# GpSimd's low halves of weights behind the first layer norm, and new constants for a written-out order

## The chip, the cores and the metric

The kernel runs on one core of a Trainium2 chip. The metric is the device time in microseconds (us) of one execution. Beside it stand readings from one profiled execution: its span, from the first to the last instruction, and the busy time of each engine. The engines are PE (matrix products), ACT (activations), DVE (vector operations), POOL (GpSimd, vector operations too, slower) and SP, which here only issues transfers.

## What is computed

A block of four residual layers over eight sequences of 512 tokens with 128 channels, everything in 32-bit floats:

```python
x = x + ssm(layernorm(x))        # 128x128 in, 3-tap convolution, a scan over 512 tokens
x = x + ffn(layernorm(x))        # 8 experts, all of them for every token
x = x + attention(layernorm(x))  # 16 heads of 8, tokens see their chunk of 10 and 25 before their own place
x = x + ffn(layernorm(x))        # the same experts again
```

The part that takes most of the time is the expert layer, used twice:

```python
g = einsum('bsh,ehf->ebsf', x, w_gate)      # 8 experts, 128 -> 512
u = einsum('bsh,ehf->ebsf', x, w_up)
h = silu(g) * u
y = einsum('ebsf,efh->ebsh', h, w_down)     # 512 -> 128
cw = softmax(x @ w_router) * softmax(x @ w_gating / 0.1)
out = einsum('ebsh,bse->bsh', y, cw / (sum(cw) + 1e-9))
```

The first layer is a scan: with `decay` and `drive` of shape (tokens, 64, 8), `state = decay * state + drive`, and the output of a token is the sum of `state * c` over the 8 states plus `D * x`.

## The kernel before

**Products.** A product of 32-bit accuracy is made of three fast ones (`matmul3`): each operand is split into a high half (a cast to the type fp32r) and a low half (what the cast left out), and high x high, low x high and high x low are summed in one bank. So each of the 24 weight tiles of the experts (`wg`, `wu`, `wd` for 8 experts) is loaded as `stage...`, its high half cast by ACT, and its low half taken by a subtraction, on GpSimd at first, on GpSimd or DVE later (`lows`, lines 987 to 1000). Every hidden tile `h` is split in the same way: `h0...` of four or two products, `h00`/`h01` its high half, `h10`/`h11` its low half.

**The order.** All instructions of all engines are written out by the program itself while it is built. `Clock` keeps, in Python, an account of when each engine would be free: `cost` says what an instruction is charged, `run` where it goes, and for transfers (key `S`) when the data would be there. `Lanes` holds generators, one per chain of work; a `yield "V", t` says that the next instructions need DVE and data that is there at `t`; a `yield` of a function waits for a condition. `tick` takes the lane that can start first. The order on each engine is then fixed, and the chip keeps to it, with semaphores between the engines. So a constant of the account changes no arithmetic, but it may change the place of any instruction on any engine.

**The stages.** The scan of sequence 0 is done first and in two halves of 256 tokens (`first_halves`, half `c` = 0 and 1), so that the expert layer can start with the first half. `scanned` is one such half: `decays` computes softplus and exponentials on ACT (`delta`, `mdec`), `clips` bounds them on DVE, `steps` multiplies and scans (`mst`), `mcx` weighs the states, and `mo` are the products of the output. Then `ffn_prep` normalises (`layernorm`: statistics `st`, `mv` on DVE, `va` and `rs` on GpSimd, `xn` on DVE), transposes (`tp`), splits (`xt0`, `xt1`), and computes the router's weights (`lps`, `rps`, `cps`, `cw`), which go to memory and come back spread over the partitions (`cwb`).

Until the first half is ready PE has nothing else to do and is kept busy with products `warm` that nobody reads (line 1750 and on). Later such products, then called `idle`, are put in by `keep_warm` when the account finds PE free for over `WARM_GAP` (0.25 us) in the first one and a half sequences.

The expert layer is one stream (`ffn_stream`): for each sequence, for each expert, for each quarter of 128 of the 512 hidden channels, a `g`, a `u` and, some steps later, a `y`, three products of 512 columns each. Of sequence 0 the first experts, `SPLIT` of them, are passed twice, with 256 tokens each time and two quarters at once (six products of 256 columns). Six banks hold `g`, `u` and `y`; the rest of the eight belong to the side chains. Beside the stream run the scans of the sequences 1 to 7 (`mamba_front`, `mamba_back`), the preparation of the next expert layer (`ffn_preps`) and the attention (`attention_preps`, then `attention`). `due` functions and `MAMBA_DUE` and `PREP_DUE` say from which position in the stream a chain is pressing, `SIDE`, `JOIN` and `JOIN_ATT` how long a chain's products wait to join others on PE, `HELD` how much a chain is held back while PE is starved.

**The gate on the low halves.** The first `EARLIEST` = 10 weight tiles have their low halves taken before the first layer norm where time allows. A set of names in `done` steers them: "halves" lets them start, "quiet" stops them. "quiet" is set when the layer norm of the first half begins to be issued, and taken away when its output is split. While "quiet" is there, the second half's DVE steps wait too (`undisturbed`).

Of the kernel before, what the change touches and what calls it, by code (L numbers as in the profile page):

```python
# [87 lines left out]

TABLES = {AF.Silu: (18,), AF.Exp: (0, 6), AF.Ln: (6,), AF.Tanh: (0, 18)}
INF = float("inf")  # L90
LAGS = {"T": 0.2, "A": 0.15, "V": 0.15, "P": 0.08}
TO_PE = 0.11
SAME = 0.125
# [1 line left out]
EDGE = 0.1  # L95
FIRST = 0.6
LATE = 0.3
SIDE = 0.5
JOIN = 2.0
JOIN_DUE = 0.0  # L100
JOIN_MAX = 6.0
JOIN_ATT = 3.0
JOIN_END = 2.0
MOST = 6
OTHERS = 4
# [3 lines left out]
WARM_TO = 1.5  # L109
SECOND = 0.2  # L110
PRESS = 0.4
HELD = 0.18
MAMBA_DUE = 0.9
PREP_DUE = 0.9
ATT_LEAD = 2.5
EARLY = 5
SPLIT = 4
EARLIEST = 2 * (DEPTH + 1)


# [8 lines left out]
class Clock:  # L129
# [105 lines left out]
    def run(self, key, name, out, args, kw, after, wait):  # L235
        c = self.cost(key, name, out, args, kw)
        start = max(self.end[key] + wait, after, self.now if key == "T" else self.based(key))
        if key == "T":
            if start > self.end["T"] + 2.4:
                self.cold = start  # L240
            if start < self.cold + 3.4:
                c *= 2
        if key in "VP" and self.shares(key, name, out, args):
            start = self.with_port(start, c)
        self.end[key] = start + c
        if key == "S":
            start = max(start, self.now)
            row = out.shape[-1]
            rows = out.shape[0] * size(out) // row
            each = max(row * (2 if out.dtype == BF16 else 4), 512)  # L250
            move = rows * each / 200e3
            self.moved = max(self.moved, start + c + 0.8) + move
            return self.moved + 0.6 + move
        self.hop[key] = start + c
        return start + c + LAGS[key]

# [23 lines left out]
class Lanes:  # L280
# [39 lines left out]
    def start(self, lane):  # L320
# [3 lines left out]
        if callable(need):  # L324
            return 0.0 if need() else INF
        if need == "T":
# [51 lines left out]
def block_kernel(ctx: ExitStack, tc: tile.TileContext, x, pack_a, pack_b, pack_c, w_qkv, mask, mask_t, w_o,  # L378
                 w_gate, w_up, w_down, out):
    nc = tc.nc  # L380
    clock = Clock()
# [21 lines left out]
    done = {}  # L403
# [163 lines left out]
    def table(name, number):  # L567
        if clock.table != number:
            nc.scalar.preload_act_table_set(name)
            clock.table = number  # L570
            clock.end["A"] = max(clock.end["A"], clock.now) + 1.28
# [63 lines left out]
    first = lambda gen: lanes.hurry(gen, FIRST)  # L635
# [69 lines left out]
    def first_halves(sb, consts, h, xo):  # L705
# [39 lines left out]
        def scanned(c, pbc, pde):  # L745
# [37 lines left out]
            def decays():  # L783
                yield "V"

                e = freed(dve.tensor_scalar(delta, pde, bdt, LN_E_1, ALU.add, ALU.min))
                yield lambda: issued["tanh"] == 2
                yield "A", e
                nega = consts["nega"]
                table("natural_log_exp_and_others", 6)  # L790
                act.activation(delta, delta, AF.Exp)
                act.activation(delta, delta, AF.Ln, bias=1.0)
                for p in range(2):
                    yield "A"
                    dec = sb.tile([P, 2, HALF], F32, tag="dec", name=f"mdec0_{c}_{p}", bufs=5)
                    for i in range(2):

                        decs["t", p, i] = act.activation(
                            dec[:, i], delta, AF.Exp, scale=nega[:, 2 * p + i : 2 * p + i + 1]
                        )  # L800
                    decs[p] = dec
                if c:
                    table("exp_and_others", 0)
# [53 lines left out]
            for p in range(2):  # L857
# [6 lines left out]
                for t in range(2):  # L864
                    for i in range(2):
                        pe.matmul(
                            ops[t], cx[:, i, t * P : (t + 1) * P], pa[:, A_WOUT : A_WOUT + P],
                            start=False, stop=(p == i == 1),
# [88 lines left out]
    def ffn_weights(sb):  # L957

        todo = [(e, nm, src) for e in range(NE) for nm, src in (("g", w_gate), ("u", w_up), ("d", w_down))]
        stages = {}  # L960

        def load(i):
            e, nm, src = todo[i]
            if i < EARLIEST:

                t = fp.tile([P, L], F32R, tag=f"h{i % 2}", name=f"stage{nm}{e}", bufs=DEPTH + 1).bitcast(F32)
            else:
                t = qp.tile([P, FF], F32, tag=("t0", "t1", "rest")[i % 3], name=f"stage{nm}{e}")
            if nm == "d":
                end = sp.dma_start(  # L970
                    out=t.rearrange("p (c h) -> p c h", c=NFC),
                    in_=src[e].rearrange("(c p) h -> p c h", p=P),
                )
            else:
                end = sp.dma_start(out=t, in_=src[e])
            stages[i] = t, end + 1.5

        def loads():
            for i in range(3, len(todo)):
                if i > EARLIEST + 2:  # L980
                    yield lambda: i - 3 in split
                    yield "S", split[i - 3]
                load(i)

        split = {}

        def lows():
            for i, (e, nm, _) in enumerate(todo):
                yield lambda: i in stages and len(stages[i]) == 3
                yield lambda: "halves" in done and "quiet" not in done if i < EARLIEST else "first" in done  # L990
                t, there, _ = stages.pop(i)
                hi, lo = wgt[nm, e]
                yield "PV" if "first" in done else "P", there
                engine = quicker(L, W_BIAS) if "first" in done else pool
                split[i] = engine.tensor_tensor(lo, t, hi.bitcast(F32), ALU.subtract)
                done[nm, e] = 0.0
            done["weights"] = 0.0

        for i in range(3):
            load(i)  # L1000
        sp.dma_start(out=pb, in_=pack_b)
        lanes.add(loads())
        lanes.add(lows())
        for i, (e, nm, _) in enumerate(todo):
            yield lambda: i in stages
            t, there = stages[i]
            if e == EARLY:
                yield lambda: "first" in done
            yield "A", there
            stages[i] = t, act.copy(wgt[nm, e][0], t), True  # L1010
# [12 lines left out]
    def ffn_prep(k, b, xc, t0=0, nt=NT):  # L1023
# [11 lines left out]
        *_, xf = yield from normalised(xc, nm, halves, nt, t0 + nt == NT, quick=nt < NT, plain=True)  # L1035
        if (k, b, t0) == (0, 0, 0):
            done.pop("quiet", None)
            done["calm"] = 0.0
        if t0 == 0:
            done["cw", k, b] = dram.tile([NE, NT, P], F32, tag="cwd", name=f"cwd_{nm}", bufs=3), 0.0, 0  # L1040
# [678 lines left out]
    with mctx:  # L1719
        sb = msb  # L1720
        mc = {}

        def late(part):
            return lambda: pos[0] >= turn[part] - MAMBA_DUE

        def fronts(seqs):
            for b in seqs:
                turn["front"] = b
                xc = first_x
                if b:  # L1730
                    xc = yield from load_x(b, 0, f"m{b}")
                    yield lambda: ("front", b - 1) in done
                yield from mamba_front(b, sb, mc, xc)
                done["front", b] = 0.0

        def backs(seqs):
            for b in seqs:
                turn["back"] = b
                yield lambda: b in handed and (b - 1, 1) in done
                yield from mamba_back(b, sb, mc, lambda gen: lanes.add(gen, due=late("back")))  # L1740

        first(fronts(range(1)))
        first(mamba_consts(sb, mc))
        lanes.add(ffn_weights(sb))
        clock.hold = INF

        warm = now(side([P, L], "warm"))
        while (0, 0) not in ready or ready[0, 0][1] == 0:
            if lanes.tick():
                continue  # L1750
            if clock.now > WARM:
                sel = mc["sel"]
                e = pe.matmul(warm[:, :HALF], sel[:, 0], sel[:, : HALF // P], start=True, stop=True)
                clock.end["T"] += 0.1
            else:
                clock.now += 0.03
        freed(e)

        done["first"] = 0.0
        lanes.add(backs(range(1, B)), due=late("back"))  # L1760
        lanes.add(fronts(range(1, B)), due=late("front"))
        lanes.add(ffn_preps(), rank=0, due=lambda: pos[0] >= turn["prep"] - PREP_DUE)
        lanes.add(attention_preps(), rank=QRANK, joins=JOIN_ATT)
        stream = ffn_stream()

        def keep_warm():

            if pos[0] < WARM_TO and clock.now > clock.end["T"] + WARM_GAP and lanes.are_free("bank"):
                t, = take("experts", [[P, L]], ["idle"])
                sel = mc["sel"]  # L1770
                freed(pe.matmul(t[:, :HALF], sel[:, 0], sel[:, : HALF // P], start=True, stop=True), "experts")

        while "weights" not in done or (B - 1, 1) not in done:
            if next(stream):
                lanes.idle()
                keep_warm()
            else:
                lanes.tick()
# [85 lines left out]
```

## Time and profile before

| | |
|---|---|
| median of 3 runs | 1352.26 us (1350.01 to 1354.05) |
| the profiled execution's own time | 1351.71 us |
| its span | 1349.9 us |
| granted clock of PE, mean | 0.996 |
| first product of the expert layer (`g`) starts at | 34.25 us |
| products of PE | 98% of the span |

A time is read as "start, duration, engine, line, operation, out<-in". Almost every instruction has line 269, as one helper issues them all; they are told apart by the names of their tiles. The names in the profile leave numbers out: `h<-h` may be any of the hidden tiles. In square brackets stands how long the engine had been idle before and what it had waited for. In the lists of waits the columns are the total, the count and the longest.

### The profile page before, as it was taken

Reading aid. Unit: us, or ns where it says so; the run is one execution under the profiler, and the core shown is the slowest. Engines: PE = TensorE matmul, PEld = TensorE weight load, DVE = VectorE, ACT = ScalarE, POOL = GpSimd, SP = SyncE. Lnnn points to the kernel's source line nnn. Section 1 sums busy time; section 2 is a strip of 40 time slices with the busy share of each in tenths; the row PEclk is TensorE's granted clock in tenths of the full one; section 3 lists DMA queues with packets and bytes.
Section 4 is the critical chain, followed back from the end, with each engine's and each line's share of the span. In section 5 each row is a group of like instructions: output and inputs, shape, how many; then the busy total and the mean of one; then the engine's idle time right before and its main releaser. Section 6 shows DMA issues by size and latency. Waiting matters only on the chain.

```text
span 1349.9 us, 29483 instructions
## 1 busy us (share of the span) xinstructions
PE 1328.8 (98%) x10261; PEld 1053.4 (78%) x10261; DVE 1038.5 (77%) x3114; ACT 964.2 (71%) x1694; POOL 941.4 (70%) x1042
## 2 busy tenths in 40 slices
PE   7999999999999999999999999999999999999998
PEld 7877778788788877777777777777777777778886
DVE  6887888688888877897788887888888787845443
ACT  7768576867787556776777777777877767765654
POOL 5877576776767757676766767767677676777776
PEclk9999999999999999999999999999999999999999
DMA  4320303232111261344344453344443434121111
GB/s 126 95 82 28 87 24 101 64 80 76 42 48 56 63 86 52 72 102 113 79 102 114 98 125 88 95 110 102 104 99 96 114 76 102 47 71 53 40 40 40
DMA packets 182204, 107.74 MB, mean 80 GB/s; under 512 B 86401, under 2 KB 162088, under 8 KB 182056
## 3 DMA queue, kind: packets, MB, share of 16 engines
q1 hardware_dynamic: 182056, 105.87, 31.6%
q8 instruction: 81, 1.33, 0.4%
q14 instruction: 67, 0.55, 0.1%
HBM read 77.64 MB, written 27.79 MB: 78 GB/s over the span
## 4 chain that ended last, share of the span: by engine, by line
PE 91%; ACT 2%; issue 2%; POOL 2%; DVE 1%; POOLq 0%; DVEq 0%
PE u L269 26%; PE g L269 25%; PE y L269 25%; PE ao L269 2%; PE aw L269 2%; PE as L269 2%; PE mo L269 1%; POOL h L269 1%; PE aqk L269 1%; ACT h L269 1%; DVE h L269 1%; PE aout L269 1%; PE mde L269 1%; PE yp L269 1%; PE tp_f L269 0%
## 5 line engine op out<-in xcount | busy, mean ns | idle before, releaser
L269 POOL TENSOR_TENSOR h<-h,h 128x512 fp32r<-128x512 f32 x492 | 639.8, 1309 | 280.0 <-ACT h L269 223.2
L269 PE MATMUL u<-xt_f,wu 128*128 128x512 f32 (+1 forms) x1584 | 451.4, 395 | 3.6 <-ACT h L269 2.7
L269 PE MATMUL g<-xt_f,wg 128*128 128x512 f32 (+1 forms) x1584 | 448.4, 393 | 2.1 <-ACT h L269 1.9
L269 PE MATMUL y<-h,wd 128*128 128x512 f32 (+1 forms) x1584 | 445.6, 392 | 1.4 <-POOL h L269 0.8
L269 DVE TENSOR_TENSOR h<-u,h 128x512 f32<-128x512 f32 x420 | 285.8, 686 | 157.7 <-PE u L269 109.8
L269 ACT ACTIVATE h<-g 128x512 f32<-128x512 f32 x512 | 303.4, 597 | 124.8 <-PE g L269 100.6
L269 ACT CAST h<-h 128x512 fp32r<-128x512 f32 x437 | 268.3, 618 | 169.2 <-DVE h L269 167.6
L269 PEld LDWEIGHTS g<-xt_f,wg 128*128 128x128 f32 x1584 | 288.5, 189 | 70.2 <-ACT h L269 3.0
L269 PEld LDWEIGHTS y<-h,wd 128*128 128x128 f32 x1584 | 288.3, 188 | 70.3 <-POOL h L269 1.5
L269 PEld LDWEIGHTS u<-xt_f,wu 128*128 128x128 f32 x1584 | 286.7, 189 | 71.5 <-ACT h L269 4.1
L269 POOL TENSOR_TENSOR acc<-acc,cwb 128x512 f32<-128x512 f32 (+1 forms) x114 | 148.0, 1298 | 52.1 <-DVE cwb L269 44.9
L269 ACT ACT_TABLE_LOAD x109 | 139.8, 1283 | 25.2 <-PE g L269 23.7
L269 DVE CUSTOM_DVE_ANT_0 amasked<-as,maskq 128x60 f32<-128x60 f32 x640 | 95.3, 213 | 4.9 <-PE as L269 4.6
L269 DVE TENSOR_TENSOR cwb<-y,cwb 128x512 f32<-128x512 f32 (+1 forms) x116 | 77.4, 668 | 14.1 <-PE y L269 13.6
L269 DVE TENSOR_TENSOR apt<-aw,maskk 125x400 f32<-125x400 f32 (+2 forms) x160 | 88.1, 570 | 0.0
L269 DVE SCALAR_TENSOR_TENSOR h<-h,g 128x512 f32<-128x512 f32 x92 | 62.3, 681 | 28.3 <-ACT h L269 27.8
L269 ACT ACTIVATE apt<-apt 125x400 f32<-125x400 f32 (+2 forms) x160 | 81.5, 540 | 0.4
L269 DVE SCALAR_TENSOR_TENSOR h<-u,h 128x512 f32<-128x512 f32 x92 | 62.5, 683 | 3.3 <-PE g L269 0.5
L269 DVE DVE_READ_ACCUMULATOR2_ANT amx<- 128x1 f32 x640 | 51.9, 81 | 0.0
L269 DVE CAST h<-h 128x512 fp32r<-128x512 f32 x75 | 50.6, 675 | 1.2
L269 DVE COPY v<-avr 125x128 f32<-125x128 f32 (+2 forms) x40 | 25.5, 638 | 26.5 <-PE ao L269 26.0
L269 PEld LDWEIGHTS ao<-apt,v 125*32 125x32 f32 (+2 forms) x1280 | 27.4, 109 | 14.6 <-DVE h L269 4.0
(205 smaller groups left out, 1241.4 us busy)
## 6 DMA issues: line engine op xcount, KB each, us to landing
cwb<-cwd_f SPq DMA_DIRECT2D x124, 256.0 KB
aqd<-apc SPq DMA_DIRECT2D x32, 192.0 KB
ks<-aqd SPq DMA_DIRECT2D x48, 93.8 KB
x_fo<-x SPq DMA_DIRECT2D x16, 256.0 KB
aqd<-apc SPq DMA_DIRECT2D x32, 128.0 KB
x_f<-x SPq DMA_DIRECT2D x15, 256.0 KB
qs<-aqd SPq DMA_DIRECT2D x48, 75.0 KB
aod<-aos SPq DMA_DIRECT2D x24, 100.0 KB
```

The lines of the kernel that those rows point to most:

```text
L269: f(*args, **kw)
```

## The change

Three things are changed.

A second name, "still", stops the first ten low halves as "quiet" does. It is set when the exponentials of half 0 are issued, so earlier than "quiet", and taken away with it. It doesn't hold the second half's DVE steps.

The account of a transfer: before, it was there at (start + issue + 0.8, or the end of the one before) + move, + 0.6 + move; now at (start + issue + 0.6, or the end of the one before) + move, + 0.8. For 256 KB `move` is 1.31 us and the issue is charged with 0.55.

The constants: a filler `warm` is charged with its own cost and 0.02 us more instead of 0.1 (`FILL`); `SIDE`, `JOIN_ATT`, `HELD`, `MAMBA_DUE`, `PREP_DUE` have new values; `SPLIT` is 5 instead of 4, so that expert 4 of sequence 0 is passed in two halves as well.

```diff
+FILL = 0.02
-SIDE = 0.5
+SIDE = 0.6
-JOIN_ATT = 3.0
+JOIN_ATT = 8.0
-HELD = 0.18
-MAMBA_DUE = 0.9
-PREP_DUE = 0.9
+HELD = 0.15
+MAMBA_DUE = 1.0
+PREP_DUE = 0.8
-SPLIT = 4
+SPLIT = 5
...
-            self.moved = max(self.moved, start + c + 0.8) + move
-            return self.moved + 0.6 + move
+            self.moved = max(self.moved, start + c + 0.6) + move
+            return self.moved + 0.8
...
+                if c == 0:
+                    done["still"] = 0.0
                 table("natural_log_exp_and_others", 6)
                 act.activation(delta, delta, AF.Exp)
...
-                yield lambda: "halves" in done and "quiet" not in done if i < EARLIEST else "first" in done
+                yield lambda: "halves" in done and not {"quiet", "still"} & done.keys() if i < EARLIEST else "first" in done
...
             done.pop("quiet", None)
+            done.pop("still", None)
...
-                clock.end["T"] += 0.1
+                clock.end["T"] += FILL
```

## The prediction

> **What bounds the kernel now.** I read the page first, then the table of windows by stage, the waits of PE, and the timeline of the first 80 us. From the page and from the windows:
>
> ```profile
> PE 1328.8 (98%) x10261; PEld 1053.4 (78%) x10261; DVE 1038.5 (77%) x3114; ACT 964.2 (71%) x1694; POOL 941.4 (70%) x1042
> ```
>
> ```profile
> 0.00:34.20 34.20, 26.89 (x175) 23.95 (x175) 21.54 (x57) 25.10 (x54) 18.62 (x29) 0.95 0.40 125
> 34.20:100.00 65.80, 62.80 (x413) 54.32 (x414) 55.30 (x121) 46.74 (x84) 51.91 (x60) 0.97 0.31 86
> 100.00:200.00 100.00, 96.15 (x438) 74.62 (x437) 77.87 (x163) 73.38 (x125) 68.29 (x73) 0.98 0.17 50
> 300.00:400.00 100.00, 100.00 (x479) 79.93 (x478) 84.28 (x163) 77.90 (x135) 67.33 (x67) 1.00 0.20 57
> ```
>
> The columns are the window, its length, the busy time of PE, PEld, DVE, ACT and POOL, and the granted clock. From 300 us on PE is never free, so a new order can win nothing there but cheaper changes of shape. What can move lies in the first 200 us, where PE idles and its granted clock falls to 0.95 to 0.98; "busy" there also counts 111 `warm` and 30 `idle` products that compute nothing. The waits of PE say who is late:
>
> ```profile
> PE u L269 <- ACT h L269: 2.7, 3, 1.5
> PE mbx L269 <- DVE mst L269: 2.6, 1, 2.6
> ```
>
> The timeline ahead of the first expert product `g` (start, duration):
>
> ```profile
> 23.33 0.80 PE L269 MATMUL mbx<-mbc,sel 128*128 128x256 f32 x2 [2.57 <-DVE mst L269]
> 24.56 1.91 PE L269 MATMUL mo<-pa,mcx 128*128 128x128 f32 x8
> ...
> 27.54 1.05 PE L269 MATMUL mo<-pa,mcx 128*128 128x128 f32 x8
> 28.34 3.00 PE L269 MATMUL warm<-sel 128*128 128x256 f32 x23
> 28.88 1.29 POOL L269 TENSOR_TENSOR wd<-staged,wd 128x512 fp32r<-128x512 f32 x1
> 29.23 0.30 DVE L269 BATCH_NORM_AGGREGATE mv_f<-st_f 128x2 f32<-128x6 f32 x2
> 30.25 0.19 POOL L269 TENSOR_SCALAR va_f<-mv_f 128x2 f32<-128x2 f32 x1
> 31.77 0.50 PE L269 MATMUL tp_f<-ident,xn_f 128*128 128x128 f32 x2 [0.43 <-DVE xn_f L269]
> ```
>
> The statistics are there at 29.53, but GpSimd starts `va_f` only at 30.25, behind the low half `wd`: 0.72 us that the new gate aims at. The eight `mo` at 24.56 take 1.91 us, those at 27.54 take 1.05: the first stand behind a wait of 2.57 us and run at half rate. Inside the first expert block:
>
> ```profile
> 61.74 0.88 PE L269 MATMUL g<-xt_f,wg 128*128 128x256 f32 x6
> 62.46 0.88 PE L269 MATMUL u<-xt_f,wu 128*128 128x256 f32 x6
> ...
> 64.53 1.28 ACT L569 ACT_TABLE_LOAD   x1
> ...
> 68.36 2.15 PE L269 MATMUL idle<-sel 128*128 128x256 f32 x5 [0.86 <-DVE cwt_f L269]
> 69.88 1.28 ACT L269 ACT_TABLE_LOAD   x1
> 70.56 1.45 PE L269 MATMUL u<-xt_f,wu 128*128 128x256 f32 x6
> 71.17 1.58 ACT L269 ACTIVATE h<-g 128x512 f32<-128x512 f32 x3
> ```
>
> Six products are 0.72 us from start to start when they flow. `g` of 61.74 gets its Silu only at 71.17, since ACT loads four tables between 61.08 and 71.16 and does the exponentials of sequence 1 between them; PE runs out of work at 68.2 and then creeps at half rate (0.43 us per `idle`, where 0.117 is usual).
>
> **The change, part by part.** The build gives the new order of every engine; durations are those of the rows above.
>
> *Gate and fillers, up to the first `g`.* Low halves `wg2`, `wu2`, `wd2` go behind the layer norm, so `va_f` no longer waits: at most 0.72 us sooner. But FILL makes fillers cheaper in the kernel's account, and `warm` goes from 111 to 159, 0.117 us each. Nine more stand ahead of the first `tp_m` and `mh`, where the chain has little slack: I take +0.2 us there and +0.1 before the first `mbx`. Twelve more stand inside the wait of 2.57 us, which leaves 1.2 us: no half rate, so `mo` is 0.86 us shorter and the second `mo` starts with its data (27.2 instead of 27.54). Then 31 instead of 23 stand before `tp_f`: 31 x 0.117 = 3.6 us from 28.2, so `tp_f` starts at 31.85 although its data is there at 31.2. The fillers eat the gate's gain. Four more before `lps` add 0.3; the four `mo` and the `idle` that now follow it (33.36 to 34.2) move behind, 0.9 less. First `g` at 33.75 instead of 34.25: **-0.5 us**; bounds -1.3 (no filler in the way) and +0.6 (no half rate saved).
>
> The skill page TensorE: Matmul & The Clock Gate, "Part 1: The HAM clock gate", puts the fall to half rate after an idle window of about 3.4 us. The row shows it after 2.57 us. By the page the fillers inside that wait would save nothing and the start would be about +0.3 us instead of -0.5.
>
> *SPLIT 5, with the new order up to expert 5.* Before, 65.3 us pass from the first `g` (34.25) to the first `g` of expert 5 (99.57). The products in them, each at its usual start-to-start time, are 288 of 256 columns at 0.117, 41 of 512 at 0.235, 16 `mo` at 0.22 and 2.5 us of small ones: 49.4 us. So 15.9 us were fillers, waits and half rate. After, the order has 342 of 256 columns, 11 of 512, 18 `mo` and about 2 us of small ones: 48.6 us. Its waits I worked out queue by queue:
> - GpSimd starts six lows at 31.5 (1.3 each), then `h10` of the first hidden tile: 40.6. The small router steps stand behind it, so `cps_f` is ready at 42.3, while PE reaches it at 40.05. This is a new wait of 2.25 us, and what is queued behind `cps_f` on PE is the first `y`. Then `mo` waits for DVE's `mcx` (46.4) and `y` for GpSimd (46.6). PE reaches the second half at about 62.1: 28.4 us for 23.1 of products, 5.3 lost, against 5.7 before.
> - From there to expert 5, 10.2 us were lost before. Now the exponentials of sequence 1 and of the router share one table load, and the Silu of the second half follows one more: two loads of 1.28 fewer in this stretch. From its own load to that Silu ACT needs 7.3 us, and PE has 8.4 us of products ahead of the first that needs the bank. Expert 4's five extra groups are that cover; without it PE would stand about 3 us as it does now. I take 1.5 us lost here, and 3.2 up to expert 5 where `wd7` and its neighbours come sooner in GpSimd's queue.
>
> Together about 10 us instead of 15.9: **-5.9**, and 0.8 fewer products. Bounds: -11 if half of the 10 goes too, +2 if the new wait costs as the one at 68 did.
>
> The skill page ScalarE: Activation LUTs, "What ACT_TABLE_LOAD costs", gives about 2.66 us per switch with its drain; the rows show 1.28 and the next activation 0.01 us behind. By the page the two loads would be worth 5.3 us instead of 2.6.
>
> *What is pushed behind.* Products of the side chains that stood before expert 5 come after it: total product time after the first `g` is 1284.9 us against 1284.6, so +1.0 from expert 5 on, and the 0.8 above is given back.
>
> *Constants in the rest.* A shape change costs PE 0.11 us (518.2 us: 0.34 to the second product of `u`, 0.232 usual). Pricing the whole order by such pairs gives -2 to +1 from the second sequence on: 0. Thirteen casts go from ACT (0.62) to DVE (0.43) under a full PE: 0. The two extra half steps of expert 4 (DVE 0.41, GpSimd 0.73, one transfer) lie beside PE.
>
> *Account of transfers.* The first `x` is issued at 0.72 and used at 3.71, 3.0 us. The account charged 4.6 and now charges 3.3, so users are queued 1.3 us sooner but not too soon. SP sends `cwd` and the `cwb` of the first half ahead of the store of `x0`; the waits of DVE, ACT and GpSimd name a DMA only for that first `x`, so 0. If that cover goes, the price is 1.3 us each time in front of DVE.
>
> Sum: -0.5 - 5.9 - 0.8 + 1.0 = -6.2 us. The waits inside the block were worked out with undisturbed durations, while DVE's clips beside a GpSimd low took 0.57 and 0.87 us instead of 0.33; for this I keep about three quarters: -4.5. The profiled execution is 1351.7 (span 1349.9 and 1.8 around it), 0.6 below the median of 1352.26. So **1347.5**; by itself 1344 to 1350.
>
> **The rivals.**
> - *GpSimd's backlog decides (slower).* Three lows, 3.9 us, now stand ahead of every `h10`. If GpSimd is the last to release PE through the first block, PE trails by 3.9 and runs 2 us longer at half rate after the wait for `cps_f`: +5.9 - 0.5 - 1.4 (12 `idle` fewer) = +4.0, 1355.7. It decides once GpSimd has under 3.9 us free before the second half; it was busy 20.6 of 26 us from 34 to 60, so 5.4 were free, which speaks against it.
> - *A new stall later (no change).* Before, one wait of 1.94 us at 174 (`u`, `g` behind ACT's exponentials) was followed by products at 0.43 instead of 0.23 up to 179: 3.9 us in all. The second sequence's side work is now denser by 1.0 us. One such stall more: 1351.
> - *All of it (faster still).* Waits fall to 5 us: 1342. For it: PE's products would allow it. Against: DVE is busy 22.4 of 26 us from 34 to 60.
> - *The gate does nothing,* as fillers hold `tp_f`: this is in my sum.
>
> **How the numbers follow.** Forecast 0.45, faster still 0.12, no change by a new stall 0.20, backlog 0.23. Runs spread by 0.3% (1350.0 to 1354.1), about what can be told from no change: 1348.2 to 1356.3 is "same". Of the forecast a quarter ends in "same", of the backlog a third: faster 0.46, same 0.34, slower 0.20; as uncounted mishaps only add time I move 0.08 from same to slower. Range 1341.5 to 1357: the bounds of the block on one side, the backlog on the other.
>
> **What would show it.** `va_f` within 0.2 us of its statistics, `tp_f` behind `warm` and not behind DVE; the `mo` before 25 us in about 1 us; first `g` near 33.75; a wait at `cps_f` near 40 to 42; the first `g` of expert 5 near 93 to 95; from 300 us on full PE in every window. I am wrong if expert 5 starts after 98, or if a wait over 1.5 us appears after 130 that was not there.

## The result, and the profile after

The changed kernel takes 1364.67 us in the median of 6 runs (1362.07 to 1365.96), the kernel before 1351.61 in 6 runs beside it: a ratio of 1.0094, 95% interval 1.0079 to 1.0108. It is 13 us slower. Forecast were 1347.5 us, with a range of 1341.5 to 1357, so the prediction was wrong.

First the lines of after that answer to those shown of before: the page's line of busy times, the windows by stage, and of PE's waits the four longest of real products for ACT and the one of `mbx`.

```profile
PE 1336.9 (98%) x10333; PEld 1059.1 (78%) x10333; DVE 1039.3 (76%) x3135; ACT 951.1 (70%) x1664; POOL 946.4 (69%) x1048
```

```profile
0.00:36.30 36.30, 32.35 (x218) 30.05 (x218) 21.20 (x55) 24.89 (x54) 15.01 (x26) 1.00 0.38 118
36.30:100.00 63.70, 58.27 (x421) 52.55 (x420) 57.76 (x119) 40.36 (x75) 51.38 (x56) 0.97 0.27 79
100.00:200.00 100.00, 97.69 (x456) 76.45 (x455) 70.67 (x147) 69.75 (x127) 69.04 (x78) 0.98 0.18 51
200.00:300.00 100.00, 95.92 (x437) 74.32 (x436) 83.81 (x160) 75.07 (x130) 68.88 (x69) 1.00 0.25 69
300.00:400.00 100.00, 98.44 (x463) 77.96 (x462) 87.59 (x168) 75.16 (x128) 67.42 (x67) 1.00 0.27 72
```

```profile
PE y L270 <- ACT h L270: 2.3, 3, 1.4
PE u L270 <- ACT h L270: 2.1, 2, 1.3
PE g L270 <- ACT h L270: 1.9, 2, 1.7
PE aw L270 <- ACT h L270: 1.7, 1, 1.7
PE mbx L270 <- DVE mst L270: 1.0, 1, 1.0
```

The share of PE is 98% in both, so the first line tells nothing. The windows do: from 300 to 400 us PE had no free time before, and now 1.6 us of it; from 200 to 300 it has 4.1, where it had 1.5 before:

```profile
200.00:300.00 100.00, 98.55 (x454) 78.77 (x453) 78.18 (x147) 73.15 (x126) 69.72 (x68) 1.00 0.30 82
```

The wait of `mbx` near 24 us fell from 2.6 to 1.0 as expected; all of PE's waits for ACT come to 11.1 us, against 7.7 before.

The start, from the timeline of after (start, duration):

```profile
6.98 2.08 PE L270 MATMUL warm<-sel 128*128 128x256 f32 x8
27.28 1.05 PE L270 MATMUL mo<-pa,mcx 128*128 128x128 f32 x8
30.58 3.96 PE L270 MATMUL warm<-sel 128*128 128x256 f32 x31
32.16 0.20 POOL L270 TENSOR_SCALAR va_f<-mv_f 128x2 f32<-128x2 f32 x1 [11.75 <-DVE mv_f L270]
34.38 0.38 PE L270 MATMUL tp_f<-ident,xn_f 128*128 128x128 f32 x2
36.34 0.98 PE L270 MATMUL g<-xt_f,wg 128*128 128x256 f32 x6
```

The gate does what it says: GpSimd is idle for 11.75 us and starts `va_f` with its data. Yet the first `g` stands at 36.34, 2.1 us later than before, in an execution whose first products went at half rate (eight `warm` took 2.08 us, and 1.19 before). Two kernels that have the same order here start it at 33.92 and 33.88, so the change does not bring the delay; the last section comes back to it.

To see where time is lost I split both runs at the first `g` of a sequence's expert 0 and of its expert 4. A stage's loss is its length less its products, each at its usual start-to-start time as in the prediction. It may be negative, where shapes flow better than their mean. Each column is one execution; the three profiles that share the changed kernel's order in the second row lose 6.2, 5.9 and 6.0 us there.

| loss of PE in us | before | after | constants alone | gate alone | new account alone | after with the old account | one nudge (`h_lag_pe`) |
|---|---|---|---|---|---|---|---|
| first `g` to sequence 1 | 17.9 | 15.4 | 13.8 | 19.2 | 19.8 | 16.0 | 15.4 |
| sequence 1, experts 0 to 3 | 1.5 | 6.2 | 8.0 | 7.8 | 7.3 | 8.6 | 6.2 |
| sequence 1, experts 4 to 7 | 3.4 | -0.3 | -0.1 | 1.1 | 2.2 | -0.1 | -0.2 |
| sequence 2, experts 0 to 3 | -0.7 | 5.2 | 5.9 | 2.0 | 0.6 | 3.0 | 5.2 |
| from there to sequence 5 | -1.0 | 0.1 | 6.3 | 11.5 | 1.8 | -0.7 | 0.1 |
| sequence 5 to the second expert layer | 1.5 | 3.6 | 1.3 | 1.3 | 2.0 | 0.8 | 2.0 |
| second expert layer | 2.8 | 7.1 | 5.3 | 6.0 | 4.7 | 5.5 | 5.0 |
| sum | 25.4 | 37.3 | 40.5 | 49.0 | 38.5 | 33.0 | 33.8 |

Before and after: the first block loses 2.5 us less, which just makes up for the late start (sequence 1's first `g` stands at 129.17 against 129.01). Then 4.7 and 5.9 us go in the two stages of experts 0 to 3, against 3.7 won between them, and some 7.5 us behind expert 4 of sequence 2. The other columns are explained below.

**What stands at 133 to 145 us.** ACT and PE in the timeline of after:

```profile
132.23 0.60 ACT L270 ACTIVATE h<-g 128x512 f32<-128x512 f32 x1 [0.96 <-PE g L270]
132.84 1.28 ACT L570 ACT_TABLE_LOAD   x1
134.14 1.30 ACT L270 ACTIVATE mdelta<-mdelta 128x512 f32<-128x512 f32 x2
135.99 1.95 ACT L270 ACTIVATE mdec<-mdelta,nega 128x512 f32<-128x512 f32 x3
138.71 1.28 ACT L270 ACT_TABLE_LOAD   x1
140.01 1.57 ACT L270 ACTIVATE h<-g 128x512 f32<-128x512 f32 x3
140.66 0.82 PE L270 MATMUL idle<-sel 128*128 128x256 f32 x2 [1.76 <-ACT h L270]
141.54 1.65 PE L270 MATMUL u<-xt_f,wu 128*128 128x512 f32 x3
```

This is the picture that the prediction showed of before at 61 to 71 us: ACT changes its table, does the exponentials of a scan, changes back, and does no Silu in between, here for 7.2 us. PE runs dry, waits 1.76 us, and then the products go at half rate, at a granted clock of 0.50 from 141.5 to 144.9 us: 1.65 us for three where 0.86 is usual. These are the decay exponentials `mdec` of sequence 2's scan. Before, they stood here:

```profile
118.95 1.28 ACT L569 ACT_TABLE_LOAD   x1
120.24 1.95 ACT L269 ACTIVATE mdec<-mdelta,nega 128x512 f32<-128x512 f32 x3
123.11 1.28 ACT L269 ACT_TABLE_LOAD   x1
```

That is within sequence 0, 8.8 us ahead of sequence 1's first `g` (129.01). In the changed kernel they come 6.8 us behind it (129.17). Those of sequence 3's scan moved from 171.0 to 211.1, from 42 us ahead of sequence 2's first `g` to 1 us ahead. Before, PE waited 1.94 us behind them, up to 176.6; after has no wait over 1.5 us there, which goes with the 3.7 us won. What the new place does on DVE shows in the timeline of after some us later:

```profile
221.85 0.62 ACT L270 CAST h<-h 128x512 fp32r<-128x512 f32 x1 [1.90 <-DVE h L270]
222.33 0.69 DVE L270 SCALAR_TENSOR_TENSOR mbx<-mdec,mbx 128x512 f32<-128x512 f32 x1
222.55 1.27 POOL L270 TENSOR_TENSOR h<-h,h 128x512 fp32r<-128x512 f32 x1 [3.48 <-ACT h L270]
223.53 1.21 DVE L270 TENSOR_TENSOR_SCAN mst<-mdec,mbx 128x512 f32<-128x512 f32 x1
223.86 0.60 ACT L270 ACTIVATE h<-g 128x512 f32<-128x512 f32 x1 [1.38 <-POOL h L270]
224.51 0.97 PE L270 MATMUL g<-xt_f,wg 128*128 128x512 f32 x3 [1.66 <-ACT h L270]
```

It is read from the bottom: PE's `g` waits for a bank that ACT empties, ACT for a hidden tile that GpSimd releases, GpSimd for ACT's cast, and the cast for DVE's `h`, while DVE works on the scan. The four scans `mst` of sequence 3 start within 12 us (216.3 to 228.3); before they were spread over 41.5 us (184.5 to 226.1).

**What stands behind 570 us.** The chain of waits of after names a transfer, `x` for the attention's layer norm, three times (start, and the time from issue to use):

```profile
569.47 6.93 DMA x_a<-x
...
829.39 6.05 DMA x_a<-x
...
917.48 6.64 DMA x_a<-x
```

The engines' waits for transfers:

```profile
DVE st_a L270 <- DMA x_a<-x: 8.3, 5, 3.2
DVE st_f L270 <- DMA x_f<-x: 2.9, 2, 2.3
DVE cwb L270 <- DMA cwb<-cwd_f: 2.6, 3, 1.1
```

All of DVE's waits for transfers come to 20.3 us, against 5.1 before, of which 3.7 is the very first load. Before's transfers of `x_a` were hardly quicker, 5.8 to 6.6 us from issue to use in the three where it can be read; but its DVE came to them later, and waited for one alone:

```profile
DVE st_a L269 <- DMA x_a<-x: 0.9, 1, 0.9
```

### The profile page after: what moved, and what is told of

It reads as the page before. It is cut to its first block, busy times and chain, and to the rows that moved or that the text cites. A ratio compares the mean times of both kernels' runs of the same rounds, so it can differ in the third digit from the quotient of the medians.

```text
span 1363.7 us, 29669 instructions
## 1 busy us (share of the span) xinstructions
PE 1336.9 (98%) x10333; PEld 1059.1 (78%) x10333; DVE 1039.3 (76%) x3135; ACT 951.1 (70%) x1664; POOL 946.4 (69%) x1048
## 4 chain that ended last, share of the span: by engine, by line
PE 87%; DVE 3%; ACT 3%; issue 2%; DMA 2%; POOL 2%; SPq 0%; POOLq 0%; ACTq 0%; DVEq 0%
PE u L270 24%; PE y L270 24%; PE g L270 24%; PE ao L270 2%; PE aw L270 2%; PE as L270 2%; DMA x_a<-x 1%; PE mo L270 1%; POOL h L270 1%; ACT h L270 1%; PE warm L270 1%; DVE h L270 1%; PE aqk L270 1%; PE yp L270 1%; ACT mdec L270 0%
## 5 line engine op out<-in xcount | busy, mean ns | idle before, releaser
L270 ACT CAST h<-h 128x512 fp32r<-128x512 f32 x424 | 260.6, 619 | 194.7 <-DVE h L270 193.4
L270 ACT ACT_TABLE_LOAD x107 | 137.3, 1283 | 28.1 <-PE g L270 24.5
L270 DVE TENSOR_TENSOR cwb<-y,cwb 128x512 f32<-128x512 f32 (+1 forms) x117 | 77.5, 663 | 14.7 <-PE y L270 10.2
L270 DVE CAST h<-h 128x512 fp32r<-128x512 f32 x88 | 54.1, 618 | 1.3
L270 PE MATMUL ao<-apt,v 125*32 125x100 f32 (+2 forms) x1280 | 36.4, 254 | 0.0
```

What stands on the lines that cost most here:

```text
L270: f(*args, **kw)
```

## The experiments

Theory A: the new account lets DVE stand in front of transfers that have not landed. Theory F: the cheaper fillers cost the start. Theory S: the constants only shuffle the order, before's order happens to be a good one, and a new one loses some us by its own stalls, whatever led to it. Later a rival C stands against S: the change's parts do harm by what they are.

### Parts taken out, or put in alone

Four kernels: the changed one with the old account of transfers, and with the old charge for fillers; the kernel before with the new account alone, and with the gate alone.

```diff
 # a_old_account, in the changed kernel
-            self.moved = max(self.moved, start + c + 0.6) + move
-            return self.moved + 0.8
+            self.moved = max(self.moved, start + c + 0.8) + move
+            return self.moved + 0.6 + move
 # a_old_fill, in the changed kernel
-FILL = 0.02
+FILL = 0.1
 # b_new_account, in the kernel before: the first hunk the other way round
 # b_gate, in the kernel before
+                if c == 0:
+                    done["still"] = 0.0
...
-                yield lambda: "halves" in done and "quiet" not in done if i < EARLIEST else "first" in done
+                yield lambda: "halves" in done and not {"quiet", "still"} & done.keys() if i < EARLIEST else "first" in done
...
+            done.pop("still", None)
```

> The changed kernel with the old account of transfers, all else as changed. Theory A (transfers charged too little put DVE in front of landings; its queue stands and PE runs dry): 6 to 9 us less than the changed kernel, about 1357, and DVE's waits for a DMA behind the first x gone. Theory F (fillers cost the start): no more than 1 us less. Theory S (every new order loses some us by its own stalls, whatever the constant): anywhere from 1350 to 1365, with stalls in places that have nothing to do with transfers.

> The changed kernel with fillers charged as before. Theory F: the first g at 33 to 34 instead of 36.3, and 2 to 3 us less, about 1362. Theory A: 0 to 2.5 less, the waits for x_a stay. Theory S: 1350 to 1365 with another set of stalls.

> The kernel before with the new account of transfers alone. Theory A: 1357 to 1361, DVE waits 5 to 15 us in all for DMAs, x_a above all. Theory F: 1351 to 1352. Theory S: 1350 to 1360, waits for DMAs no more than one in three of the loss.

> The kernel before with the earlier gate on the low halves alone. Theories A and F: va_f starts within 0.2 us of its statistics, first g 0.3 to 0.9 us sooner, 1350 to 1352. Theory S: up to 5 us from before either way, by stalls behind the first g.

| kernel | median, us | ratio to before (95%) | DVE's waits for transfers, us |
|---|---|---|---|
| after, old account | 1360.91 | 1.0068 (1.0053 to 1.0083) | 5.7 |
| after, old charge for fillers | 1361.80 | 1.0070 (1.0055 to 1.0085) | 17.9 |
| before, new account | 1366.63 | 1.0103 (1.0082 to 1.0125) | 20.1 |
| before, gate | 1374.83 | 1.0168 (1.0136 to 1.0201) | 6.4 |

The account's waits follow the account. With the new one in the kernel before:

```profile
DVE st_a L269 <- DMA x_a<-x: 9.5, 6, 2.4
DVE cwb L269 <- DMA cwb<-cwd_f: 5.1, 3, 2.3
```

and with the old one in the changed kernel:

```profile
DVE st_a L270 <- DMA x_a<-x: 0.8, 2, 0.4
```

The five kernels with the new account wait 16.9 to 22.4 us in all, the fifteen with the old one 4.9 to 10.2. So theory A is right that the new account puts DVE in front of transfers. It is not the whole: the old account gives back 3.8 us of 13, where theory A expected 6 to 9, and the gate, which has nothing to do with it, costs 23 us alone. The old charge for fillers gives 2.9 us, what theory F expected. The new account alone and the gate alone came out above every range that was stated for them, theory S included (1361 and 1357 at most). The parts cost 14 and 23 us alone and 13 together with all others, so these numbers belong to the orders that came out and not to the parts.

### The order held, one part put in

To see a part's direct effect, the planner keeps its books as before and only the emitted instructions differ. Gate: the three low halves `wg2`, `wu2`, `wd2` are charged where they stood, and emitted behind the copy of `va_f`; nothing but GpSimd's queue changes. Fillers: 46 more `warm` (111 become 157), not charged; nothing but PE's queue changes.

```diff
 # e_gate_fixed
-                split[i] = engine.tensor_tensor(lo, t, hi.bitcast(F32), ALU.subtract)
+                if i in (6, 7, 8):
+                    split[i] = engine.charge("tensor_tensor", lo, t, hi.bitcast(F32), ALU.subtract)
+                    moved_lows.append((lo, t, hi.bitcast(F32), ALU.subtract))
+                else:
+                    split[i] = engine.tensor_tensor(lo, t, hi.bitcast(F32), ALU.subtract)
...
+            if tag == "f0_0_0":
+                for args in moved_lows:
+                    nc.gpsimd.tensor_tensor(*args)
 # e_fill_fixed, behind each filler
+                fills += 1
+                if fills > 19 and fills % 2:
+                    nc.tensor.matmul(warm[:, :HALF], sel[:, 0], sel[:, : HALF // P], start=True, stop=True)
```

> The order before is kept on every engine and transfer queue but GpSimd's, where only the low halves of wg2, wu2 and wd2 move from ahead of the first layer norm's copy, subtraction and power to just behind them; the planner's books are as before. What it tells is the gate's own direct effect, without a new order. By the prediction's step on the start: the statistics end at about 32, so the first product `g` comes at most as early as the full gate brought it, 1.7 us sooner (32.51 against 34.25 in the run with the gate alone); the three lows come about 1.5 to 2 us later, and expert 2's first use is not until some 20 us on, so nothing waits for them. Theory S (the gate is harmless or a small gain, and the 23 us that it cost alone are a new order's stalls far behind): 1350 to 1352, 0 to 1.7 us faster than before. Its rival G (lows taken late hold up the experts after): over 1356.

> The order before is kept on every engine, and only TensorE gets more fillers: behind every second filler from the 20th on one more, which the planner is not charged for (111 fillers become 157). Theory F (more fillers of 0.07 to 0.13 us each delay real work at the start, as in the changed kernel, where the first `g` comes 2.1 us later): the first `g` comes 1 to 3 us later and the time goes up by as much, 1353 to 1355. Theory S (fillers fit into gaps that the order leaves; the changed kernel's late start comes from its other order there): the first `g` within 0.7 us of 34.25 and the time within 0.7 us of before, 1351 to 1352.5. A granted clock that stays higher in the first 30 us could make it 0.5 us faster.

Gate: 1351.22 us, ratio 1.0006 (0.9994 to 1.0017). Fillers: 1352.04 us, ratio 0.9998 (0.9989 to 1.0006). Neither interval leaves out 1. Four of the gate's twelve executions took about 1356 us, at a mean granted clock of 0.994 where the others have 0.996 to 0.999, and what sets them apart is not on record.

The first `g` came at 35.76 with the gate and at 37.51 with the fillers, 1.5 and 3.3 us behind the 34.25 of before. But in both the first 11 us went at half rate, as in `e_press`, a kernel with before's order there (next part), whose first `g` stands at 36.51: against that one the gate brings it 0.75 us forward and the fillers put it 1.0 back, in one execution each. By sequence 2 the delay against before is 1.2 and 1.5 us, and the medians don't show it. So fillers may delay the start by about a microsecond, as theory F has it, but the time doesn't go up by as much.

The account of transfers and the five constants that only steer the planner can do nothing at a held order. `SPLIT` also changes the shapes of products, and no run held the order for it. So gate, fillers and account cost nothing by themselves that the medians show: what they cost, they cost through the order that is written. For `SPLIT` that is not shown.

### Nudges that mean nothing

Nine kernels are the one before with one number of the planner moved a little, two are the changed kernel so moved.

```diff
-PRESS = 0.4            # e_press, and f_after_press
+PRESS = 0.41
-AHEAD = 0.2            # e_ahead, and f_after_ahead
+AHEAD = 0.205
-SIDE = 0.5             # f_before_side
+SIDE = 0.52
-HELD = 0.18            # g_held
+HELD = 0.185
-start + c + 0.8) + move          # g_account_nudge
+start + c + 0.81) + move
-MAMBA_DUE = 0.9        # g_mamba
+MAMBA_DUE = 0.91
-LAGS = {"T": 0.2, "A": 0.15, "V": 0.15, "P": 0.08}
+LAGS = {"T": 0.21, "A": 0.15, "V": 0.15, "P": 0.08}    # h_lag_pe; 0.19 in h_lag_pe_down
+LAGS = {"T": 0.2, "A": 0.15, "V": 0.16, "P": 0.08}     # h_lag_dve
```

> Before, with one planner constant that the change does not touch moved by a fortieth: PRESS 0.4 to 0.41. The order is that of before up to about 110 us and another one behind. Theory S (before's order is one that came out well among many alike, and any new order costs some us by its own stalls, whatever led to it): 1355 to 1370, and new TensorE waits of 1 to 3 us in places behind 110 us. Theory A (before's constants are good, and the loss is owed to what the change does to them, to the account of transfers above all): within 3 us of before, 1349 to 1355.

> Before, with another planner constant that the change does not touch moved by a fortieth: AHEAD 0.2 to 0.205. The order is that of before up to about 115 us. Theory S: 1355 to 1370, with TensorE waits in other places than in the other changed orders. Theory A: 1349 to 1355.

Beside them, the two nudges of the changed kernel, a third nudge of before, and the change's six order constants alone in the kernel before:

```diff
 # f_constants
-SIDE, JOIN_ATT, HELD, MAMBA_DUE, PREP_DUE, SPLIT = 0.5, 3.0, 0.18, 0.9, 0.9, 4
+SIDE, JOIN_ATT, HELD, MAMBA_DUE, PREP_DUE, SPLIT = 0.6, 8.0, 0.15, 1.0, 0.8, 5
```

> The changed kernel with PRESS 0.4 to 0.41, the same nudge that cost the kernel before 11.6 us. The order is that of the changed kernel up to about 300 us. Theory S (before's order is a well come out one; the changed kernel's is an ordinary one among its like): a nudge has nothing good to lose here, so it goes either way, 1357 to 1369, within about 8 us of the changed kernel's 1364.7. Rival C (a nudge always costs, as it did before, and the change costs its own 13 us on top): 1370 to 1377.

> The changed kernel with AHEAD 0.2 to 0.205, the nudge that cost the kernel before 5.2 us. The order is that of the changed kernel up to about 545 us, with the 8 us that it had lost by then, so less is left to move: theory S 1359 to 1368, on either side of 1364.7. Rival C: 1369 to 1372.

> The kernel before with SIDE 0.5 to 0.52, a fifth of the change's step in that constant; the order is that of before up to about 165 us. Theory S: 1354 to 1365, as for the two other nudged neighbours (1357.1 and 1363.5). Rival C: 1350 to 1354.

> The kernel before with the six order constants of the change alone (SIDE 0.6, JOIN_ATT 8, HELD 0.15, MAMBA_DUE 1.0, PREP_DUE 0.8, SPLIT 5); gate, fillers' charge and account of transfers as before. The prediction's steps on the constants (the new order of the first block, worth 5.9, and nothing in the rest) would give 1345 to 1348, with the first `g` of expert 5 near 93 to 95. Theory S: 1355 to 1370, whatever the first block gains.

> The kernel before with HELD 0.18 to 0.185, against the direction of the change (0.15). The order leaves that of before at about 60 us. Theory S (any early departure from before's order lands on an ordinary order): 1360 to 1375. Rival C (the change's parts do harm by what they are; a nudge that means nothing costs little): 1350 to 1357.

> The kernel before with 0.81 for 0.8 in the account of transfers, where the change has 0.6 (and 0.8 for 0.6 plus the move behind it). The account stays as true or untrue as it was; the order leaves that of before at about 110 us. Theory S: 1355 to 1370, and few waits for transfers, unlike the new account's 14 us of them on VectorE. Rival C: 1350 to 1356, so that the new account's 15 us would be its own.

> The kernel before with MAMBA_DUE 0.9 to 0.91, a tenth of the change's step. The order leaves that of before at about 130 us. Theory S: 1354 to 1368. Rival C: 1350 to 1356.

> The kernel before with the lag of a hand-over from TensorE taken as 0.21 for 0.2 in the planner. The order leaves that of before at the same instructions as the change's constants did (about 42 us). If leaving it early is what costs: 1362 to 1376. If the parts of the change harm by what they are: 1349 to 1360, as the six nudges before.

> The kernel before with the lag of a hand-over from VectorE taken as 0.16 for 0.15. The order leaves that of before at about 60 us. If leaving it early costs: 1360 to 1376; if the parts harm by what they are: 1349 to 1360.

> The kernel before with the lag of a hand-over from TensorE taken as 0.19 for 0.2. The order leaves that of before at about 58 us. If leaving it early costs: 1360 to 1376; if the parts harm by what they are: 1349 to 1360.

In the table, the third column says when ACT does `mdec` of sequence 2's scan, counted from sequence 1's first `g`; the fourth what PE loses in sequence 1, experts 0 to 3; the fifth and sixth the same for sequence 3's scan and sequence 2.

| kernel | median, us; ratio (95%) | `mdec` 2 | lost | `mdec` 3 | lost |
|---|---|---|---|---|---|
| before | 1352 | -8.8 | 1.5 | -42 | -0.7 |
| `g_mamba` | 1349.14; 0.9970 (0.9961 to 0.9980) | -8.8 | 1.0 | -33 | -0.5 |
| `h_lag_pe_down` | 1351.32; 0.9995 (0.9986 to 1.0005) | -4.5 | 2.1 | -28 | 1.2 |
| `f_before_side` | 1353.46; 1.0009 (0.9999 to 1.0018) | -8.8 | 1.5 | -41 | -0.7 |
| `g_account_nudge` | 1354.75; 1.0020 (1.0011 to 1.0029) | -9.3 | 0.8 | -39 | 1.0 |
| `g_held` | 1356.66; 1.0033 (1.0020 to 1.0046) | -4.4 | 2.2 | -28 | 1.2 |
| `e_ahead` | 1357.12; 1.0039 (1.0027 to 1.0052) | -4.4 | 2.2 | -28 | 1.2 |
| `h_lag_dve` | 1358.91; 1.0053 (1.0037 to 1.0069) | -3.2 | 4.4 | -34 | -0.6 |
| `h_lag_pe` | 1362.66; 1.0069 (1.0054 to 1.0084) | +10.4 | 6.2 | +3.9 | 5.2 |
| `e_press` | 1363.46; 1.0083 (1.0070 to 1.0096) | -3.8 | 1.9 | -38 | -0.5 |
| after | 1364.67; 1.0094 (1.0079 to 1.0108) | +6.8 | 6.2 | -1 | 5.2 |
| `f_after_press` | 1363.65; 1.0094 (1.0071 to 1.0117) | +6.8 | 5.9 | -1 | 5.6 |
| `f_after_ahead` | 1360.07; 1.0061 (1.0042 to 1.0079) | +6.8 | 6.0 | -1 | 5.7 |
| after, old account | as above | +4.1 | 8.6 | -16 | 3.0 |
| after, old fillers | as above | +10.4 | 8.4 | -21 | 2.0 |
| new account alone | as above | +10.6 | 7.3 | -26 | 0.6 |
| gate alone | as above | +3.7 | 7.8 | -26 | 2.0 |
| constants alone | 1368.79; 1.0122 (1.0103 to 1.0142) | +12.0 | 8.0 | -2 | 5.9 |

Three readings.

Theory S is half right. A nudge that means nothing moves this kernel by -4 to +11 us, 4.5 in the median (ratio times 1352), and six of nine are slower beyond their intervals. By the ranges stated ahead, three of the nine came out as S (or an early departure) would have it, five as its rival would, and `g_mamba` below both. The kernels with parts of the change lose 8 to 23 us, and only two nudges reach into that. On the changed kernel the nudges cost nothing (the same and 4.6 us less), as S said and C did not. The last three nudges were made to ask whether leaving before's order early is what costs: `h_lag_pe`, which leaves it within a few instructions of where the constants do, loses 9.3 us, as early departure would have it; the other two lose 7.2 and nothing, as they would if the parts themselves did harm. So an early departure can cost as much as a part, but does not have to.

What goes with the loss in the two stages is where the exponentials stand. With `mdec` of sequence 2 ahead of sequence 1's first `g` the stage loses 0.8 to 4.4 us, with it behind 5.9 to 8.6, in all 18 rows without exception, whichever part or nudge led to it. Some kernels share an order: it is 14 different ones in sequence 1, and 13 in sequence 2. For sequence 3 it is a slope: 28 us ahead or more -0.7 to 1.2, 16 to 26 ahead 0.6 to 3.0, up to 2 us ahead or behind 5.2 to 5.9. The constants alone show it most plainly. They do a good part of what the prediction said of the first block: the first `g` of expert 5 at 96.52 instead of 99.57 (93 to 95 was expected), and that of sequence 1 at 124.02 instead of 129.01. Then, from PE's waits between 129 and 172 us,

```profile
PE idle L269 <- ACT h L269: 2.3, 4, 0.7
PE idle L269 <- DVE mst L269: 1.6, 1, 1.6
```

and at expert 4 this kernel and the one before are level, 172.06 against 172.01. In the end it is over 16 us slower, where the prediction's steps gave 4 to 7 us faster. This is a going-together in many orders, and a chain of waits that shows how. No run moved these exponentials alone with all else held, so it is not shown as the cause in the strict sense.

The rest does not follow from that. `e_press` loses 13 us between 253 and 450 us and the gate alone 11.5 there, with waits of `u` for ACT's `h` of up to 2.7 us. The longest are the same picture once more: in `e_press` PE's waits of 2.3 and 2.7 us end at 341.3 and 403.5, 5 to 6 us behind exponentials of a scan (335.8 and 397.6) with a table load on either side. But before does the like at 313.2 to 319.9 us and PE waits for nothing there, so such a stretch does not always stop PE, and what makes it do so stays open. So does why each part of the change lets sequence 2's scan come late.

`g_mamba` beats both kernels: 1349.14 us, 0.3% under before. It is a find by chance, one of nine, not a gain that was understood.

## Why the prediction was wrong, point by point

By stages of the two profiled executions, after less before: the first `g` came 2.1 us later (forecast -0.5); from there to expert 5 it took 1.3 us less (forecast 6.7 less, with the products); from expert 5 to sequence 1 it took 0.7 less (forecast up to 1.0 more); from sequence 1 to PE's end it took 14.1 us more (forecast 0, for the constants and the account). With the constants alone, from sequence 1 on, it is 20.0 us more. So the step that failed is "Constants in the rest, 0": an order priced by pairs of neighbouring products has no waits in it. The first block's gain, mis-sized at -5.9, would have made up for less than half of that.

- **Start, -0.5.** As a mechanism right: `va_f` 0.1 us behind its statistics, `tp_f` behind `warm`, the eight `mo` in 1.05 us. The rule of the Trainium skill weighed there (TensorE: Matmul & The Clock Gate, "Part 1: The HAM clock gate") would have had the fillers in the 2.57 us wait save nothing; with the wait cut to 0.98 us, `mo` fell from 1.91 to 1.05, as the row of before said and the rule did not. The first `g` at 36.34 belongs to that one execution: the two nudged changed kernels have the same order there and start `g` at 33.92 and 33.88, where 33.75 was forecast. What failed is that this was put into the sum: by expert 5 the 36.34 and the 33.92 have become 100.39 and 100.55, so even 2.4 us at the start are worth nothing in these.
- **SPLIT 5 and the first block, -5.9.** About half right for the constants alone: from the first `g` to expert 5 they take 62.1 us instead of 65.3, where 6.7 less was forecast, and sequence 1's first `g` comes 5.0 us sooner (the loss falls by 4.1). In the changed kernel nothing of it is left in the times: expert 5 at 100.39 to 100.55 in the three profiles with this order, not 93 to 95, and sequence 1 at 129.2 to 129.3 against 129.0. The table loads near 60 us fell as said; instead of one wait of 2.25 us at `cps_f` there were two of 0.91, for DVE's `mst` up to 40.59 and for its `h` up to 44.41. Which of gate, fillers and account takes the constants' 5 us away was not tried; the gate alone has sequence 1 at 129.57, although its first `g` stands at 32.51.
- **What is pushed behind, +1.0.** For PE's products up to sequence 1 there is nothing to see of it (0.7 us less from expert 5 on). What it left out is the ACT and DVE work that moves too. The exponentials of sequence 2's scan, with their table loads, had their place in sequence 0; now they hold the Silus for 7.2 us behind 133 us, and those of sequence 3's scan stand later as well. The losses of the stages from sequence 1 to expert 4 of sequence 2 change by +4.7, -3.7 and +5.9 us. That these exponentials are the cause goes with all the orders tried and with the chain of waits, and was not isolated. The table load itself took 1.28 us here too, with the next activation 0.02 us behind it.
- **Constants in the rest, 0.** Wrong, and the largest miss. Pricing the order by pairs of neighbouring products sees changes of shape and no wait. It gave -2 to +1 from the second sequence on, and measured was +14.1, with the constants alone +20.0. The 14.1 are the stages of the point above and, behind expert 4 of sequence 2, a loss that rose by 7.5 us. Of those 7.5 the waits for transfers are a part whose size no run separates; for the rest the cause stays open.
- **Account of transfers, 0.** Wrong. I took the first `x` as the measure: 3.0 us from issue to use, against a charge of 4.6 before and 3.3 now. That load is the first in the queue. In the chain `x` for the attention takes 6.0 to 6.9 us behind other transfers, so what an empty queue is charged is short, and the new charge is shorter; what the account made of the queue for these transfers is not on record. The reading that the waits name a transfer only for the first `x` held for the longest waits: the whole list of before has DVE's 0.9 us for `x_a` too. I named the price (1.3 us in front of DVE each time) and then did not charge it; DVE's five waits for `x_a` come to 8.3 us, up to 3.2 each. The old account in the changed kernel gives 3.8 us back, though through another order.
- **The rivals.** GpSimd's backlog did not decide: the first block lost less than before. "A new stall later" was the right kind, but it had one stall of 3.9 us against the gain where there are several, and ended in no change. Both of the signs that I named as proof against me came: expert 5 behind 98, and waits of PE over 1.5 us behind 130 (1.76 ahead of 140.66 and 1.66 ahead of 224.51, both shown above, and 1.73 of `aw` ahead of 582.7).
- **Chances.** A change that re-plans the order had 0.28 for slower. Of the nudges, which have no sense at all, 5 of 9 are slower by over 0.3%.

## What to carry to other kernels

Where a program plans the order of all engines, a changed constant is a new order, and its gain must be judged against what a meaningless nudge does to the same kernel (here -4 to +11 us); hold the order and change only the emitted instructions to get a part's own effect. Work that vanishes from a stage has to be looked for in the next one, on every engine and not only on the one that bounds: table changes and exponentials that leave a stage with slack may land in one without. A transfer's time should be read from a loaded queue, not from the first load.

## What was not expected of the hardware

**The first 36 us are not the same from one execution to the next.** The kernel before, `e_press` and `g_mamba` have the same instructions in the same order up to 100 us, and their first `g` stands at 34.25, 36.51 and 37.25. The windows of before, `e_press` and `g_mamba` (the third column from the end is PE's granted clock):

```profile
13.00:20.00 7.00, 6.84 (x48) 5.75 (x48) 3.41 (x7) 6.58 (x15) 3.31 (x3) 1.00 0.37 110
```

```profile
0.00:13.00 13.00, 10.67 (x50) 10.06 (x51) 5.74 (x19) 7.05 (x15) 7.60 (x18) 1.00 0.86 268
```

```profile
13.00:20.00 7.00, 5.69 (x21) 4.19 (x22) 3.56 (x7) 5.03 (x13) 3.81 (x3) 0.57 0.37 109
```

Where before does 48 products from 13 to 20 us, `g_mamba` does 21 at a clock of 0.57. `e_press` loses 2.2 us ahead of 13 us with a granted clock of 1.00 in its row: its eight `warm` took 2.06 us where before's took 1.19, so that column does not show all of it. The trace's record of the clock begins only where full speed is first granted, and the column counts what lies ahead as full. In the 20 profiled executions of this case it begins at 5.5 to 6.5 us (twelve, before among them), at 7.0 to 7.2 (three, `g_mamba` among them) or at 11.3 to 11.8 (five, `e_press` and after among them). The first `g` stands at 32.5 to 35.0 in the twelve and at 35.1 to 37.5 in the others, though their orders differ too.

The length of one wait doesn't settle whether the clock falls: PE's wait of 1.80 us up to 12.99 in before was followed by the row above at 1.00, and after's of 1.76 us up to 140.66 by 3.4 us at 0.50. The 3.0 us of `g_mamba` are still there at sequence 1 (131.91 against 129.01); from 138 us on its order is another one.

**A vector operation of DVE can take twice its time and more.** Two clips `mdec` took 2.20 us in after while GpSimd worked, and one 0.47 shortly after, when GpSimd had stood idle up to 217.63. Not every clip beside GpSimd is slow (0.48 us at 137.3), so what decides is not shown:

```profile
210.90 1.41 POOL L270 TENSOR_TENSOR acc<-acc,cwb 128x512 f32<-128x512 f32 x1
211.83 2.20 DVE L270 TENSOR_SCALAR mdec<-mdec,cap 128x512 f32<-128x512 f32 x2 [0.68 <-ACT mdec L270]
212.27 1.48 POOL L270 TENSOR_TENSOR h<-h,h 128x512 fp32r<-128x512 f32 x1
217.46 0.47 DVE L270 TENSOR_SCALAR mdec<-mdec,cap 128x512 f32<-128x512 f32 x1
```

An account of costs that charges each operation one price can't see this, and the order that it writes stands on it.
